# Setting up the second layer's weights beside the first layer's last feed-forward groups

## The chip, the cores and the metric

The kernel runs on one core of a Trainium2 chip. The metric is the device time of one execution in microseconds (us). Engines are called as the profile calls them: PE (TensorE; PEld is its weight load), DVE (VectorE), ACT (ScalarE), POOL (GpSimd) and SP (SyncE, which here only issues transfers).

## The reference

Two layers act on x (32 graphs of 512 nodes with 256 features, float32) with a 0/1 adjacency of 512 x 512 for each graph. Each layer adds a graph layer and a feed-forward layer, both on a layer norm of x:

```python
# layer 0
x = x + relu(mean_over_neighbours(ln(x) @ W_msg) + ln(x) @ W_upd + bias)
t = max_d(ln(x)[d] + Wt[f, d]) + bt                # "tropical" product, f = 0..1023
fused = g * bend(t) + (1 - g) * gelu(ln(x) @ Wc)   # g = sigmoid(ln(x) @ Wg), bend piecewise linear
x = x + fused @ Wd + bd
# layer 1
x = x + graph_attention(ln(x), adj)                # 4 heads of 64, softmax over neighbours
sw = softmax((ln(x) @ W_x.T + b_x) @ W_slice.T + b_slice) / temperature)   # 8 heads, 64 slices
x = x + (sw.T-weighted sums of ln(x) @ W_fx.T, mixed by a small recurrence, spread by sw) @ out_w.T
```

Before layer 1 can start, its weights are put into the form that the products want: W_fx and four other matrices are loaded by row blocks and transposed, W_x and W_slice are multiplied together, some norms are compared with limits.

## The kernel before

**Layer 0** is `layer0_sorted`. The 32 graphs form four segments of eight (segments 0 to 3). A generator `all_convs`, held in the variable `ahead`, does the graph convolution of a segment (`conv_in`, `conv_out`) and ends each segment with `put_in_order`. That function ranks all rows of the segment by how much work their tropical product needs and scatters the 32 row tiles `keep[t]` to a DRAM buffer `by_rank` in rank order, with 32 indirect DMAs on POOL's queue (L440). All these buffers come from a pool `sa`.

A second generator, `feed_forwards`, takes each sorted segment in eight groups (0 to 7). For a group, `sums` loads the rows (`xs`, L469 on SP), normalizes and transposes them, and gathers table rows on POOL (`rows`, L499) for the tropical maximum on DVE (`best`). `mixed` does the two products with Wc and Wg (clsp and gatep, L524 on PE), their ACT functions, the transposed tropical part (tz, L531) and the bends (`past` on ACT, `acc` on DVE). `down` multiplies by Wd (po, L551), adds on DVE (L553) and stores the rows to `x2s[s]` (L554 on SP). In the order of instructions, group g's `down` stands after the first step of group g+1's `mixed`, and the rest of `mixed` is interleaved with `sums` of the group after.

The two generators are interleaved by a helper, `woven(a, na, b, nb)`: it takes steps from a and b in the proportion na to nb, so the order of instructions on each engine is the order in which the generators are stepped. The stream `ahead` runs ahead by 32 steps and more; its last step, `put_in_order` of segment 3, comes while group 5 of segment 2 is begun, with eleven groups still to be finished.

**Layer 1** is `layer1_plain`, called when layer 0 is done. It opens its constants' pool `c1` and its PSUM pool `p1`, and does the setup:

- loads `wa` and, in a small pool `raw0`, the vectors a_dst and a_src (L813), which go into `wa` and a norm (`prod` on DVE, norm2p on PE, L820);
- loads some twenty small constants (L789);
- in a pool `raw`, calls `load_T` five times (L881, L882): a row block is loaded, each 128 x 128 part is transposed on PE (wfxp, inp, hop, owp, fcp: 72 in all) and copied on DVE;
- makes `wsl`, the product of W_x and W_slice (wslp, L922), compares norms, and takes the exponential of `ebsl`.

Then pools `s1` and others are opened and pairs of graphs go through attention and the slice mixer. `prepare` gathers the rows of a graph from `x2s` by their ranks (`x`, L960 on POOL), normalizes them and turns the adjacency (`ai`) into a mask; the first products of `attention` are avp (L1025).

Pools may lie on the left or the right end of the core's SBUF. A pool that is opened on memory which an earlier pool has given back waits, at its first uses, for all users of the memory given back. With `reuse_waits="tile"` a buffer waits only for those whose own bytes it takes.

Of the kernel before, what the change touches and what calls it, by code (L numbers as in the profile page):

```python
# [8 lines left out]
F32 = mybir.dt.float32  # L9
# [6 lines left out]
PSUM = bass.MemoryType.PSUM  # L16
DRAM = bass.MemoryType.DRAM

P = 128
N = 512  # L20
# [59 lines left out]
        live = [s for s in live if next(s, live) is not live]  # L80


def layer0_sorted(tc, ident, eps, x, adj, w, x2s, ranks, over):

# [3 lines left out]
    nc = tc.nc  # L90
# [22 lines left out]
    with ExitStack() as ctx:  # L113
        cst = ctx.enter_context(tc.tile_pool(name="c0", bufs=1))
# [36 lines left out]
        keys = dr.tile([FFN], F32, tag="keys", name="keys", bufs=1)  # L151
        sorted_rows = dr.tile([FFN, 4 * D + NF], F32, tag="sorted", name="sorted_rows", bufs=1)

        sa = ctx.enter_context(tc.tile_pool(name="sa", bufs=2))

        def bounds(raw):

# [411 lines left out]
        def all_convs():  # L569
            for s in range(len(x2s)):  # L570
                yield from convs(s)
                yield s

        ahead = all_convs()
        with tc.tile_pool(name="r0", bufs=1) as raw:
            bounds(raw)
            first = iter(lambda: next(ahead), 0)
            for _ in woven(first, SEG * 12, features(raw), 40):
                pass
        sb = ctx.enter_context(tc.tile_pool(name="s0", bufs=2))  # L580

        for _ in range(LEAD):
            next(ahead)
# [166 lines left out]
            feed_forward(g, xg, xnT, acc)  # L750


def layer1_plain(tc, ident, eps, x2s, ranks, adj, w, out, over):


    nc = tc.nc
# [20 lines left out]
    SMALL_S, SMALL_B = 50.0 * 50.0 / D, 20.0  # L777

    with ExitStack() as ctx:
        cst = ctx.enter_context(tc.tile_pool(name="c1", bufs=1))  # L780
        dr = ctx.enter_context(tc.tile_pool(name="d1", bufs=2, space=DRAM))
        ps = ctx.enter_context(tc.tile_pool(name="p1", bufs=4, space=PSUM))

        def ctile(name, shape):
            return cst.tile(shape, F32, tag=name, name=name)
# [4 lines left out]
            return t  # L790

        def psum(tag, name):
            return ps.tile([P, N], F32, tag=tag, name=name, bufs=4)

        ones = ctile("ones", [P, P])
        nc.gpsimd.memset(ones, 1.0)
# [6 lines left out]
        for c in range(DC):  # L803
            nc.sync.dma_start(wa[:, c, : AH * HO].rearrange("p (h e) -> p h e", h=AH),
                              w["W"][:, c * P : (c + 1) * P, :].rearrange("h p e -> p h e"))
        with tc.tile_pool(name="raw0", bufs=1) as raw:
            prod = raw.tile([P, DC, AH, HO], F32, tag="prod", name="prod")
            norm2 = raw.tile([P, DC, 2, AH], F32, tag="norm2", name="norm2")
            for i, name in enumerate(("a_dst", "a_src")):
                dst = wa[:, :, AH * (HO + i) : AH * (HO + i + 1)]  # L810
                vec = raw.tile([P, AH, HO], F32, tag=name, name=name)
                for h in range(AH):
                    nc.sync.dma_start(vec[:, h, :], w[name][h, 0, :].partition_broadcast(P))  # L813
                for c in range(DC):
                    nc.vector.tensor_mul(prod[:, c], wa[:, c, : AH * HO].rearrange("p (h e) -> p h e", h=AH), vec)
                nc.vector.tensor_reduce(dst, prod, AX.X, ALU.add)
                nc.vector.tensor_mul(norm2[:, :, i, :], dst, dst)
            pn = psum("mm", "norm2p")
            for c in range(DC):
                nc.tensor.matmul(pn[:, : 2 * AH], ones, norm2[:, c].rearrange("p i h -> p (i h)"),  # L820
                                 start=c == 0, stop=c == DC - 1)
            nc.vector.tensor_scalar(over[:, : 2 * AH], pn[:, : 2 * AH], SMALL, None, ALU.is_gt)
        edges = ctile("edges", [P, 2, B * NT])
        abias = const("abias", [P, AH * HO], w["gnn_bias"].rearrange("h e -> (h e)").partition_broadcast(P))
        gamma = const("gamma", [P, AH * HO], w["ln_gamma"].rearrange("h e -> (h e)").partition_broadcast(P))
# [41 lines left out]
        owT = ctile("owT", [P, KC, D])  # L867
        fcT = ctile("fcT", [P, KC, H])

        with tc.tile_pool(name="raw", bufs=2) as raw:  # L870

            def load_T(dst, src, name):

                R, Ccols = src.shape
                for r0 in range(0, R, P):
                    n = min(P, R - r0)
                    t = raw.tile([P, Ccols], F32, tag=f"raw{Ccols}", name=f"{name}_{r0}")
                    nc.sync.dma_start(t[:n], src[r0 : r0 + n, :])
                    for c in range(Ccols // P):
                        pt = psum("tp", f"{name}p{r0}_{c}")  # L880
                        nc.tensor.transpose(pt[:, :n], t[:n, c * P : (c + 1) * P], ident[:n, :n])  # L881
                        nc.vector.tensor_copy(dst[:, c, r0 : r0 + n], pt[:, :n])  # L882

            load_T(wfxT, w["W_fx"], "wfx")
            load_T(inT, w["hy_in_w"], "in")
            load_T(hoT, w["hy_out_w"], "ho")
            load_T(owT, w["out_w"], "ow")
            load_T(fcT, w["hy_fcD_w"], "fc")
            norm = raw.tile([P, KC], F32, tag="norm", name="norm")
            nc.sync.dma_start(norm, w["hy_norm_w"].rearrange("(c p) -> p c", p=P))  # L890
            for c in range(KC):
                nc.vector.tensor_scalar_mul(hoT[:, c, :], hoT[:, c, :], norm[:, c : c + 1])

            def twice_T(src, name):

                R, Ccols = src.shape
                t = raw.tile([P, 2, Ccols], F32, tag="twice", name=name)
                for i in range(2):
                    nc.sync.dma_start(t[:R, i, :], src)
                pt = psum("tp", f"{name}p")  # L900
                nc.tensor.transpose(pt[:, :R], t[:R].rearrange("p i c -> p (i c)"), ident[:R, :R])
                return pt


            wsT = raw.tile([P, G], F32, tag="wsT", name="wsT")
            nc.vector.tensor_copy(wsT, twice_T(w["W_slice"], "ws")[:, :G])
            wx = raw.tile([P, KC, D], F32, tag="wx", name="wx")
            nc.sync.dma_start(wx, w["W_x"].rearrange("(k p) d -> p k d", p=P))
            bx = raw.tile([P, KC], F32, tag="bx", name="bx")
            nc.sync.dma_start(bx, w["b_x"].rearrange("(k p) -> p k", p=P))  # L910
            bsl = raw.tile([1, H, G], F32, tag="bsl", name="bsl")
            bs = raw.tile([1, G], F32, tag="bs", name="bs")
            nc.sync.dma_start(bs, w["b_slice"].rearrange("(o n) -> o n", o=1))
            for c in range(DC + 1):
                M = P if c < DC else 1
                for i in range(H // KC):

                    half = slice(i * C, (i + 1) * C)
                    px = psum("mm", f"wslp{c}_{i}")
                    for k in range(KC):  # L920
                        lhs = wx[half, k, c * P : (c + 1) * P] if c < DC else bx[half, k : k + 1]
                        nc.tensor.matmul(px[:M, k * G : (k + 1) * G], lhs, wsT[half, :], start=True, stop=True)  # L922
                    px = px[:M, : KC * G].rearrange("p (k g) -> p k g", k=KC)
                    rt = rtemp[:M, i :: H // KC].unsqueeze(2).to_broadcast([M, KC, G])
                    if c < DC:
                        nc.vector.tensor_mul(wsl[:, c, i :: H // KC, :], px, rt)
                    else:
                        dst = bsl[:, i :: H // KC, :]
                        nc.vector.tensor_add(dst, px, bs.unsqueeze(1).to_broadcast([1, KC, G]))
                        nc.vector.tensor_mul(dst, dst, rt)  # L930
            wsl = wsl.rearrange("p c h g -> p c (h g)")
            nc.sync.dma_start(bsl_row.rearrange("(o n) -> o n", o=1), bsl.rearrange("p h g -> p (h g)"))
            nc.sync.dma_start(ebsl, bsl_row.partition_broadcast(P))
            pn = psum("mm", "norm2s")
            for c in range(DC):
                sq = raw.tile([P, H * G], F32, tag="wsl2", name=f"wsl2_{c}")
                nc.vector.tensor_mul(sq, wsl[:, c, :], wsl[:, c, :])
                nc.tensor.matmul(pn, ones, sq, start=c == 0, stop=c == DC - 1)
            most = raw.tile([P, 3], F32, tag="most", name="most")
            nc.vector.tensor_reduce(most[:, 0:1], pn, AX.X, ALU.max)  # L940
            nc.vector.tensor_reduce(most[:, 1:2], ebsl, AX.X, ALU.max)
            nc.vector.tensor_reduce(most[:, 2:3], ebsl, AX.X, ALU.min)
            for i, limit, op in ((0, SMALL_S, ALU.is_gt), (1, SMALL_B, ALU.is_gt), (2, -SMALL_B, ALU.is_lt)):
                nc.vector.tensor_scalar(over[:, 2 * AH + i : 2 * AH + i + 1], most[:, i : i + 1], limit, None, op)
            nc.scalar.activation(ebsl, ebsl, AF.Exp)

        sb = ctx.enter_context(tc.tile_pool(name="s1", bufs=2))

        def wide(tag, name, bufs):
            return sb.tile([P, N], F32, tag=tag, name=name, bufs=bufs)  # L950
# [939 lines left out]
def tile_kernel(ctx, tc, ins, out):  # L1890
# [21 lines left out]
    with tc.tile_pool(name="few", bufs=1) as few:  # L1912
# [1 line left out]
        NSEG = 4  # L1914
        x2s = [dram.tile([len(x2) // NSEG * N, D], F32, tag=f"x2s_{i}", name=f"x2s_{i}") for i in range(NSEG)]
        ranks = few.tile([P, len(x2) * NT], I32, tag="ranks", name="ranks")
        layer0_sorted(tc, ident, eps2, ins["x"], ins["adj"], w0, x2s, ranks, over[:, :n0])
        layer1_plain(tc, ident, eps, x2s, ranks, ins["adj"], w1, out, over[:, n0:])


        ones = few.tile([P, 1], F32, tag="ones", name="ones")
# [43 lines left out]
```

## Time and profile before

| what | us |
|---|---|
| runs: median (lowest to highest of three) | 5609.2 (5591.56 to 5611.99) |
| the profiled execution's own time | 5599.06 |
| its span | 5597.3 |
| PE busy | 4349.1 (78%) |
| DVE busy | 3780.8 (68%) |
| ACT busy | 1815.2 (32%) |
| POOL busy | 1458.0 (26%) |
| first scatter of segment 3 (L440) issued | 2224.18 |
| last scatter of segment 3 issued | 2339.75 |
| stores of segment 2, groups 4 to 7 (L554) | 2238.14, 2300.17, 2359.76, 2429.50 |
| last store of layer 0 | 2859.41 |
| first avp of layer 1 | 2958.85 |

The mean granted PE clock is 0.86 of full speed. Times of instructions are from the start of the span of one profiled execution; busy time is the sum over the instructions of an engine, so the busy shares are averages over parts of the kernel that have different limits. "Idle before" an instruction is put down to the semaphore event that came last.

### The profile page before, as it was taken

The page shows a single profiled execution, that of the slowest core. Times are in us where ns is not written, and L with a number is a line of the kernel's source. Part 1 is how long each engine was busy: PE and PEld are TensorE (multiplying, and loading weights), DVE is VectorE, ACT ScalarE, POOL GpSimd, SP SyncE. Part 2 cuts the span into 40 slices and gives each one's busy share as a digit, 9 for nine tenths or more (in the row PEclk, how much of TensorE's full clock was granted, in tenths as well). Part 3 has the DMA queues.
Part 4 walks back from the last instruction along what each step waited for, and adds up shares of the span by engine and source line. Part 5 has one row for each costly group of instructions (what it writes and reads, how often), then busy time and mean ns, then how long its engine had stood idle before and what let it go on. Part 6 is the DMA issues. An engine that isn't in the chain of part 4 may idle for free.

```text
span 5597.3 us, 59701 instructions
## 1 busy us (share of the span) xinstructions
PE 4349.1 (78%) x20723; PEld 3036.2 (54%) x20723; DVE 3780.8 (68%) x8934; ACT 1815.2 (32%) x3827; POOL 1458.0 (26%) x1658
## 2 busy tenths in 40 slices
PE   5565887867877778879968778788777878877787
PEld 3442554544554555445546666566566656656664
DVE  7667776878868777687856565665665566565553
ACT  1102332423333333434524233333333333333332
POOL 2244334333344333443311111111111111111110
PEclk8787988989998899989976888889888888888888
DMA  3325333344334333454422110111111011111100
GB/s 106 113 79 199 110 125 115 126 150 136 121 114 150 131 106 99 142 193 133 132 88 67 33 38 29 42 46 46 44 33 38 31 38 46 46 44 33 35 20 13
DMA packets 235116, 474.32 MB, mean 85 GB/s; under 512 B 38299, under 2 KB 114075, under 8 KB 234804
## 3 DMA queue, kind: packets, MB, share of 16 engines
q0 software_dynamic: 80256, 282.38, 15.4%
q1 hardware_dynamic: 154548, 188.02, 10.9%
q8 instruction: 166, 2.72, 0.2%
q14 instruction: 146, 1.20, 0.1%
HBM read 413.16 MB, written 57.16 MB: 84 GB/s over the span
## 4 chain that ended last, share of the span: by engine, by line
PE 31%; DVE 10%; ACT 6%; DMA 4%; issue 4%; POOL 3%; SPq 0%; DVEq 0%; POOLq 0%; ACTq 0%
PE avp L1025 9%; PE lgp L1071 3%; PE outp L1296 3%; PE yTp L1083 2%; PE oTp L1276 2%; PE zp L1128 2%; POOL sw L1073 1%; PE xp L1135 1%; DMA rows<-table,xs 1%; DVE att L1019 1%; PE vp L1287 1%; ACT swT L1090 1%; PE yp L1245 1%; PE po L551 1%; PE hp L990 1%
## 5 line engine op out<-in xcount | busy, mean ns | idle before, releaser
L1019 DVE SCALAR_TENSOR_TENSOR att<-own,other,mask 128x512 f32<-128x512 f32 x512 | 404.2, 803 | 346.0 <-PE avp L1025 336.8
L524 PE MATMUL clsp<-xnT,wc 128*128 128x512 f32 x1024 | 540.8, 646 | 107.1 <-ACT gate L526 72.5
L1025 PEld LDWEIGHTS avp<-hv,att 128*128 128x128 f32 x4096 | 522.1, 208 | 25.8 <-issue 14.4
L551 PE MATMUL po<-wd,acc 128*128 128x256 f32 x2048 | 484.2, 394 | 61.3 <-DVE acc L542 23.6
L1025 PE MATMUL avp<-hv,att 128*128 128x65 f32 x4096 | 525.5, 291 | 6.0 <-DVE att L1019 5.9
L499 POOL DMA_INDIRECT rows<-table,xs x332 | 409.7, 1234 | 426.3 <-DVE best L503 165.4
L524 PE MATMUL gatep<-xnT,wg 128*128 128x512 f32 x1024 | 496.0, 603 | 0.1
L551 PEld LDWEIGHTS po<-wd,acc 128*128 128x128 f32 x2048 | 398.6, 198 | 142.6 <-DVE xs L553 30.6
L538 DVE SCALAR_TENSOR_TENSOR acc<-past,fld,acc 128x512 f32<-128x512 f32 x448 | 353.0, 791 | 43.2 <-ACT past L537 34.2
L960 POOL DMA_INDIRECT x<-x2s,ranks x128 | 134.3, 1049 | 915.2 <-DVE rs L1030 632.3
L533 ACT ACTIVATE acc<-tz,fld 128x512 f32<-128x512 f32 x256 | 198.9, 777 | 482.8 <-PE tz L531 419.9
L531 PE MATMUL tz<-ident,best 128*128 128x128 f32 x1024 | 179.9, 291 | 202.4 <-DVE best L505 164.4
L505 DVE SCALAR_TENSOR_TENSOR best<-rows,xs,best 128x1024 f32<-128x1024 f32 x212 | 273.5, 1290 | 88.1 <-DMA rows<-table,xs 86.9
L524 PEld LDWEIGHTS clsp<-xnT,wc 128*128 128x128 f32 x1024 | 189.9, 204 | 263.6 <-issue 121.2
L524 PEld LDWEIGHTS gatep<-xnT,wg 128*128 128x128 f32 x1024 | 198.3, 197 | 230.8 <-issue 203.6
L526 ACT ACTIVATE gate<-gatep,fld 128x512 f32<-128x512 f32 x256 | 175.9, 687 | 431.7 <-DVE acc L541 238.2
L381 PE MATMUL pm<-h,adj 128*128 128x257 f32 x1024 | 279.6, 415 | 39.8 <-DVE u L387 26.0
L531 PEld LDWEIGHTS tz<-ident,best 128*128 128x128 f32 x1024 | 130.2, 147 | 326.0 <-DVE best L505 150.8
L537 ACT ACTIVATE past<-tz,fld 128x512 f32<-128x512 f32 x448 | 289.5, 692 | 28.6 <-DVE acc L538 27.6
L526 ACT ACTIVATE cls<-clsp,fld 128x512 f32<-128x512 f32 x256 | 176.2, 688 | 353.8 <-DVE acc L542 171.0
L1071 PE MATMUL lgp<-wsl,x4T 128*128 128x512 f32 x512 | 263.1, 649 | 35.7 <-ACT x4T L57 21.6
L381 PEld LDWEIGHTS pm<-h,adj 128*128 128x128 f32 x1024 | 206.7, 208 | 104.7 <-issue 32.8
(381 smaller groups left out, 8676.2 us busy)
## 6 DMA issues: line engine op xcount, KB each, us to landing
adji<-in_adj SPq DMA_DIRECT2D x128, 256.0 KB, 2.9
ai<-in_adj SPq DMA_DIRECT2D x128, 256.0 KB, 2.7
own<-ownd SPq DMA_DIRECT2D x128, 256.0 KB, 3.7
xs<-by_rank SPq DMA_DIRECT2D x32, 550.0 KB, 3.9
x<-in_x SPq DMA_DIRECT2D x32, 512.0 KB, 4.9
x2s<-xs SPq DMA_DIRECT2D x32, 512.0 KB, 2.9
out<-x SPq DMA_DIRECT2D x32, 512.0 KB, 2.9
rows<-table,xs POOLq DMA_INDIRECT x332, 5.5
```

The costliest lines, as they stand in the source:

```text
L381: nc.tensor.matmul(pm[:, : D + 1], a[:, i, t * P : (t + 1) * P], h[:, i, :], start=i == 0, stop=i == NT - 1)
L499: nc.gpsimd.indirect_dma_start(out=row, out_offset=None, in_=table, in_offset=bass.IndirectOffsetOnAxis(ap=idxs[:, k : k + 1].bitcast(U32) ...
L505: nc.vector.scalar_tensor_tensor(m, row, vals[:, k : k + 1], m, ALU.add, ALU.max)
L524: nc.tensor.matmul(pf, wf[:, c, f * P : (f + 1) * P], xnT[:, c, :], start=c == 0, stop=c == DC - 1)
L526: nc.scalar.activation(o, pf, fn, bias=fld[:, f, bf : bf + 1], scale=1.0 if fn == AF.Gelu else 0.5)
L531: nc.tensor.transpose(pt[:, t, :], best[t][:, f * P : (f + 1) * P], ident)
L537: nc.scalar.activation(r, z, AF.Relu, bias=fld[:, f, AT + b : AT + b + 1])
L538: nc.vector.scalar_tensor_tensor(y, r, fld[:, f, CH + b : CH + b + 1], y, ALU.mult, ALU.add)
L551: nc.tensor.matmul(po[:, :D], acc[f][:, t * P : (t + 1) * P], wd[:, f, :], start=f == 0, stop=f == FC - 1)
L1019: nc.vector.scalar_tensor_tensor(e, own[h], other[:, j, h : h + 1], mask[:, j, :], ALU.max, ALU.mult)
L1025: nc.tensor.matmul(pv[:, t * HE : (t + 1) * HE], att[j][:, t * P : (t + 1) * P], hv[:, j, h, :], start=j == 0, stop=j == NT - 1)
L1071: nc.tensor.matmul(pf, xnT[:, c, t * P : (t + 1) * P], wsl[:, c, :], start=c == 0, stop=c == DC - 1)
```

## The change

The pool `sa` goes to the right end of SBUF and is closed when the stream of convolutions ends. The stream then goes on with the setup of layer 1, so that the setup's instructions are interleaved with the feed-forward groups that remain. For that, `layer1_plain` becomes a generator: it yields after the a_dst/a_src part, after each row block of `load_T` and each part of `wsl`, and yields True when the setup is done; its remainder is run after `layer0_sorted`. Its setup takes PSUM buffers from layer 0's pool (`ps`, two buffers for each tag). Its pools `c1`, `raw0` and `raw` lie at the right end, in the memory that `sa` gave back. `c1`, `s0`, `s1` and `p1` get `reuse_waits="tile"`; `raw0` and `raw` keep the default waits. `load_T` puts up to four transposes into one PSUM buffer and copies them with one ACT instruction.

```diff
-        sa = ctx.enter_context(tc.tile_pool(name="sa", bufs=2))
+        aside = ctx.enter_context(ExitStack())
+        sa = aside.enter_context(tc.tile_pool(name="sa", bufs=2, side="right"))
...
             for s in range(len(x2s)):
                 yield from convs(s)
                 yield s
+            aside.close()
+            yield from following(ps)
...
-        sb = ctx.enter_context(tc.tile_pool(name="s0", bufs=2))
+        sb = ctx.enter_context(tc.tile_pool(name="s0", bufs=2, reuse_waits="tile"))
...
-def layer1_plain(tc, ident, eps, x2s, ranks, adj, w, out, over):
+def layer1_plain(tc, ident, eps, x2s, ranks, adj, w, out, over, ps):
...
-        cst = ctx.enter_context(tc.tile_pool(name="c1", bufs=1))
+        cst = ctx.enter_context(tc.tile_pool(name="c1", bufs=1, side="right", reuse_waits="tile"))
-        ps = ctx.enter_context(tc.tile_pool(name="p1", bufs=4, space=PSUM))
...
-            return ps.tile([P, N], F32, tag=tag, name=name, bufs=4)
+            return ps.tile([P, N], F32, tag=tag, name=name)
...
-        with tc.tile_pool(name="raw0", bufs=1) as raw:
+        with tc.tile_pool(name="raw0", bufs=1, side="right") as raw:
...
             nc.vector.tensor_scalar(over[:, : 2 * AH], pn[:, : 2 * AH], SMALL, None, ALU.is_gt)
+        yield
...
-        with tc.tile_pool(name="raw", bufs=2) as raw:
+        with tc.tile_pool(name="raw", bufs=2, side="right") as raw:
...
-                    for c in range(Ccols // P):
-                        pt = psum("tp", f"{name}p{r0}_{c}")
-                        nc.tensor.transpose(pt[:, :n], t[:n, c * P : (c + 1) * P], ident[:n, :n])
-                        nc.vector.tensor_copy(dst[:, c, r0 : r0 + n], pt[:, :n])
+                    pt = psum("tp", f"{name}p{r0}").rearrange("p (c r) -> p c r", r=P)
+                    cs = Ccols // P
+                    for c in range(cs):
+                        nc.tensor.transpose(pt[:, c, :n], t[:n, c * P : (c + 1) * P], ident[:n, :n])
+                    nc.scalar.copy(dst[:, :, r0 : r0 + n], pt[:, :cs, :n])
+                    yield
...
                         nc.vector.tensor_mul(dst, dst, rt)
+                yield
...
-        sb = ctx.enter_context(tc.tile_pool(name="s1", bufs=2))
+        yield True
+        ps = ctx.enter_context(tc.tile_pool(name="p1", bufs=4, space=PSUM, reuse_waits="tile"))
+        sb = ctx.enter_context(tc.tile_pool(name="s1", bufs=2, reuse_waits="tile"))
...
-        layer0_sorted(tc, ident, eps2, ins["x"], ins["adj"], w0, x2s, ranks, over[:, :n0])
-        layer1_plain(tc, ident, eps, x2s, ranks, ins["adj"], w1, out, over[:, n0:])
+        rest = []
+
+        def following(ps):
+            rest.append(layer1_plain(tc, ident, eps, x2s, ranks, ins["adj"], w1, out, over[:, n0:], ps))
+            return iter(lambda: next(rest[0]), True)
+
+        layer0_sorted(tc, ident, eps2, ins["x"], ins["adj"], w0, x2s, ranks, over[:, :n0], following)
+        for _ in rest[0]:
+            pass
```

More of the change, by code (lines that the diff above doesn't have):

```diff
@@ L80, in braid, with layer0_sorted @@
         live = [s for s in live if next(s, live) is not live]
-def layer0_sorted(tc, ident, eps, x, adj, w, x2s, ranks, over):
+def layer0_sorted(tc, ident, eps, x, adj, w, x2s, ranks, over, following):
     nc = tc.nc
@@ L878, in load_T @@
                     nc.sync.dma_start(t[:n], src[r0 : r0 + n, :])
-                    for c in range(Ccols // P):
-                        pt = psum("tp", f"{name}p{r0}_{c}")
-                        nc.tensor.transpose(pt[:, :n], t[:n, c * P : (c + 1) * P], ident[:n, :n])
-                        nc.vector.tensor_copy(dst[:, c, r0 : r0 + n], pt[:, :n])
[L884 to L888, printed above, removed]
+                    pt = psum("tp", f"{name}p{r0}").rearrange("p (c r) -> p c r", r=P)
[4 more added lines that the diff above has]
+                    yield
+            yield from load_T(wfxT, w["W_fx"], "wfx")
+            yield from load_T(inT, w["hy_in_w"], "in")
+            yield from load_T(hoT, w["hy_out_w"], "ho")
+            yield from load_T(owT, w["out_w"], "ow")
+            yield from load_T(fcT, w["hy_fcD_w"], "fc")
             norm = raw.tile([P, KC], F32, tag="norm", name="norm")
```

## The prediction

> **What bounds the kernel now.** I read the windows around the place where layer 1 begins, then the chain of waits, then the queues of GpSimd (POOL) and SyncE (SP) where the setup is to go. First the windows (us, busy time of PE, PEld, DVE, ACT, POOL with counts, PEclk, DMA share, GB/s):
>
> ```profile
> 2238.00:2300.00 62.00, 47.84 (x163) 28.91 (x162) 40.87 (x59) 21.36 (x34) 34.63 (x32) 0.89 0.46 148
> 2810.00:2862.00 52.00, 48.01 (x177) 30.25 (x175) 30.98 (x50) 22.59 (x36) 2.04 (x10) 1.00 0.08 26
> 2862.00:2890.00 28.00, 9.21 (x36) 6.55 (x36) 10.84 (x44) 1.49 (x2) 0.00 (x0) 0.53 0.49 127
> 2890.00:2920.00 30.00, 20.25 (x97) 14.31 (x97) 15.27 (x60) 0.00 (x0) 0.00 (x0) 0.50 0.26 77
> ```
>
> The last feed-forward groups keep PE 92% busy at full clock; the next 58 us have PE busy for 29.5, at half clock. That is layer 1's setup. The chain of waits names its limit:
>
> ```profile
> 2862.01 5.39 DMA beta<-in_L_gnn_ln_beta
> 2870.77 4.80 DMA wfx<-in_L_ffn_W_fx
> 2880.47 2.84 DMA in<-in_L_ffn_hy_in_w
> 2883.45 1.10 PE inp L881 x4
> 2910.97 5.66 PE wslp L922 x43
> 2924.67 0.96 POOL x L960
> 2958.85 6.29 PE avp L1025 x32
> ```
>
> Weights arrive in 2.6 to 2.8 us, two row blocks in flight, and 1.1 us of transposes lies between. The setup runs from 2858.9 to 2924.0, **65 us**, and another 34.9 pass until the first attention product (avp).
>
> Where the setup is to go, POOL does the scatters of the last sort:
>
> ```profile
> 2224.18 1.02 POOL L440 DMA_INDIRECT by_rank<-keep,ranks  x1 [14.68 <-DVE ranks L438]
> 2227.07 1.01 POOL L440 DMA_INDIRECT by_rank<-keep,ranks  x1 [1.86 <-DMA by_rank<-keep,ranks]
> 2229.97 0.97 POOL L440 DMA_INDIRECT by_rank<-keep,ranks  x1 [1.90 <-DMA by_rank<-keep,ranks]
> 2232.75 0.97 POOL L440 DMA_INDIRECT by_rank<-keep,ranks  x1 [1.81 <-DMA by_rank<-keep,ranks]
> ```
>
> Each scatter waits until the one before has landed. And SP, around that time:
>
> ```profile
> 2238.14 0.36 SPq L554 DMA_DIRECT2D x2s<-xs  x1
> 2241.39 0.36 SPq L469 DMA_DIRECT2D xs<-by_rank  x1
> 2342.80 1.30 SPq L813 DMA_DIRECT2D a_dst<-in_L_gnn_a_dst  x3
> ```
>
> The a_dst load of layer 1 already leaves in mid-layer 0, and only when the 32nd scatter (issued at 2339.75) has landed: its pool raw0 lies where the conv's buffers lay. It hurts nobody, as SP has no urgent work behind it.
>
> [...]
>
> **The change part by part.**
>
> *1. The setup leaves the boundary.* Minus 65. The layer-1 prologue follows the last store directly. Its 34.9 us contain 16 gathers of x (L960) at 1.25 us, from 2924.7 to 2938.1 and landing some 3 us later, which POOL could issue only after the setup (it waited 63.4 us for "over"). In the changed program they stand after the last row gathers of the feed-forward, on a POOL that is busy for 2 of 52 us; so they are done by its end, and what held ACT's third layer norm to 2942.2 is gone. The adjacency loads (2.7 to 5.4 us each, two in flight) then set the pace: about 28 us. Minus 6 or 7. Together **−71**; bounds −64 (prologue no quicker) and −80 (14 of the 34.9 go).
>
> *2. The setup beside groups 5 to 7 of segment 2 (both counted from 0).* The conv stream ends with the 32 scatters; at its next step the pool is closed and raw0 opened on it. raw0 kept its default waits, so its a_dst loads wait for all users of the given-back bytes: the last scatters. New is what is queued behind. In the changed program:
> - POOL has all 32 scatters back to back, ahead of the memset of "ones" and of group 6's row gathers. 2224.2 + 31 × 2.88 (the spacing above) = 2313.5, landed 2.7 later: **2316**. From 2.78 apiece: 2313; at segment 0's 3.34 ((426.54 − 323.09)/31, conv work between them): 2330.
> - SP has behind a_dst: a_src, some twenty small constants, the first row blocks of weights, group 4's store (L554) and group 6's load (L469).
> - PE has norm2p (L820), which needs ones, a_dst and a_src, ahead of po of group 4 (L551) and all later work; DVE has prod (L815) ahead of group 4's adds and group 5's acc; ACT waits for the temperature load ahead of group 5's "past".
>
> PE's work before norm2p (clsp and gatep of 5_0 to 5_2) ends near 2231. So **all four engines stand from 2231 to 2316 and beyond**. Then: eight a_dst/a_src loads (3.5 us to issue, 2.9 to land) 2322.6; prod, sums, norm2p, 2324.6; small loads on SP (10 us of issue in the old setup) until 2330, first wfx block landed (4.8 to 5.2) 2335.5, for which PE stops in mid-po; the remaining 20 po matmuls at 0.44 us, 2345; group 4's store 2346 instead of 2238.1: +108.
>
> After that some comes back. From 2238 to 2430 PE was busy 155 of 192 us (62, 60 and 70 us of windows: 47.8, 51.8, 55.5), so 37 were free; the setup's PE work, 29.5 at half clock, takes 15 to 20. A stretch bound by PE alone would regain 17 to 22; DVE (64 of 70 us busy in group 7), the weight loads in pairs of 4 us and head-of-line transposes leave about half: −8. **Shift of the feed-forward's end: +100**, bounds +85 (all regained, short scatters) and +125 (3.34 per scatter, nothing regained).
>
> *3. load_T with one copy on ACT for up to four transposes.* 72 DVE copies of 0.29 us (21 us of DVE) become 20 ACT copies. ACT is 36 to 43% busy there: nothing. ACT loads two tables more and Gelu's again, 1.28 each: hidden by the same slack[...].
>
> *4. Tile waits of s0, c1, s1, p1.* The first xs load at 429.2 follows the last scatter of segment 0 (426.54 plus landing) in both: nothing at the start. s1 and p1 are in part 1. No other order changes in the steady layers. From 2960 to 3040 the clock is 0.50 with PE 79% busy; I expect that to stay[...].
>
> **Sum**: 100 − 71 = **+29** on the profiled execution's own 5599.06: 5628. That one lies 10 below the median of 5609.2 (runs 5591.6 to 5612.0), from which it would be 5638. Between them, **5633**. About 0.5% (28 us) is what a measurement of this kernel can tell from no change.
>
> **Rivals.**
> - *The wait is short, and the kernel faster* (the other side). If scatters without row gathers among them went faster, the stall would shrink: the gain of 71 pays for a shift of 71, reached when the spacing is (2316 − 29 − 2.7 − 2224.2)/31 = 1.94 us or less. For: POOL is busy 1.0 us per scatter, and the row gathers follow one another at 1.25. At 1.27, 32 of them land by 2266, and the net is −21 (5588 by the median). If the wait were met in time altogether, the setup would hide in PE's 37 free us and leave −71 + 15 = −56 (5553). Against: four consecutive spacings of 2.8 to 2.9 with the releaser "DMA by_rank", and 95 waits on it in the whole trace. 0.14 for both.
> - *The stall spreads.* Nothing comes back, the weight loads come serially after the stall, and group 6, whose gathers also stand behind the scatters, ends up with +125 to +130: net +55 to +60, 5664 to 5669. For: SP issues in order, and group 6's load waits for group 4's store. Against: PE's free share later. 0.22.
> - *The setup doesn't move.* If the waits put the setup's bulk after the last group anyway, only the stall or only a few us remain: within ±15 of 5609. Against: the stream's steps are drawn by the weave, eight groups before the end. 0.06.
> - The forecast itself, +10 to +45: 0.58.
>
> **How the numbers follow.** The forecast's own range is 5615 to 5655; with the spread of the two bases and the spread rival it goes to 5672; downwards to 5588, the short-wait case. Slower by over 0.5% (above 5637): somewhat over half of the forecast's case (0.34 of 0.58) and the spread rival (0.22), 0.56. Within: the rest of the forecast and the unmoved setup, 0.30. Faster: the short wait, 0.14.
>
> **What would show it.** Right: PE, DVE and ACT idle from about 2231 to 2320, put down to a_dst, a_src or by_rank; 32 scatters at 2.9 us without a gather between them; group 4's store near 2346; gathers of x before the last po; first avp some 28 us after the last x2s store, without wfxp, inp and wslp between. Wrong: scatters closer than 2 us; group 4's store before 2270; the last store less than 75 us later than 2859.4; or a prologue that is as long as before.

## The result, and the profile after

The changed kernel takes 5635.8 us (median of four runs, 5634.9 to 5642.0) against 5606.3 of the kernel before measured beside it (four runs, 5591.6 to 5612.0): a ratio of **1.0059, 95% interval 1.0038 to 1.0080**. The forecast was 5633. The profiled execution has a span of 5640.2 us against 5597.3, and the difference of 42.9 us can be read in three parts (from here on, "the first avp" is the very first of these products on PE, at 2955.15 in the kernel before; the 2958.85 of the table ahead of the prediction is a later one):

| stretch | before | after | difference |
|---|---|---|---|
| start to the last store of layer 0 | 2859.4 | 2960.9 | +101.5 |
| last store to the first avp | 95.7 | 27.0 | −68.7 |
| first avp to the end | 2642.2 | 2652.3 | +10.1 |

The first row is the stall. These are windows of the changed kernel (us, busy time of PE, PEld, DVE, ACT, POOL with counts, PEclk, DMA share, GB/s):

```profile
2222.00:2228.00 6.00, 5.91 (x15) 2.35 (x13) 0.00 (x0) 2.66 (x3) 2.25 (x3) 1.00 0.13 48
2228.00:2323.00 95.00, 0.00 (x0) 0.00 (x0) 3.18 (x8) 0.00 (x0) 30.87 (x40) 0.51 0.15 51
2323.00:2343.00 20.00, 18.32 (x74) 15.34 (x74) 4.43 (x13) 4.71 (x10) 0.00 (x0) 0.84 0.37 90
2343.00:2396.00 53.00, 47.90 (x191) 30.41 (x192) 39.78 (x59) 27.22 (x45) 19.42 (x15) 0.94 0.55 172
```

For 95 us PE and ACT do nothing at all and DVE works for 3 us, while POOL is busy for a third of the time. POOL's timeline (start, duration, idle time before and its releaser) says with what:

```profile
2222.02 1.02 POOL L441 DMA_INDIRECT by_rank<-keep,ranks  x1 [14.87 <-DVE identb L803]
2224.81 0.99 POOL L441 DMA_INDIRECT by_rank<-keep,ranks  x1 [1.77 <-DMA by_rank<-keep,ranks]
...
2312.29 0.97 POOL L441 DMA_INDIRECT by_rank<-keep,ranks  x1 [2.26 <-DMA by_rank<-keep,ranks]
2313.26 0.22 POOL L799 MEMSET ones<- 128x128 f32 x1
```

Thirty-two scatters without a row gather among them, 90.3 us from the first to the last: 2.91 us each, of which 1.0 is busy. Only then do SP's loads leave, and PE's next matmul (norm2p) runs at 2323.3. SP:

```profile
2315.01 1.76 SPq L816 DMA_DIRECT2D a_dst<-in_L_gnn_a_dst  x4
...
2343.15 0.37 SPq L555 DMA_DIRECT2D x2s<-xs  x1
2346.09 0.36 SPq L470 DMA_DIRECT2D xs<-by_rank  x1
```

The store at 2343.15 is that of group 4 (2238.14 before), and the load at 2346.09 that of group 6 (2241.39 before). The waits between 2228 and 2345 (total, times, longest) put a name on each engine:

```profile
ACT nega L844 <- DMA nega<-in_L_ffn_hy_A_log: 105.6, 1, 105.6
DVE prod L818 <- DMA a_src<-in_L_gnn_a_src: 97.7, 1, 97.7
...
PE norm2p L823 <- DMA beta<-in_L_gnn_ln_beta: 95.3, 1, 95.3
POOL by_rank L441 <- DMA by_rank<-keep,ranks: 58.4, 30, 2.7
```

ACT, DVE and PE have a single wait of some 100 us each; the longest single wait of the kernel before in this stretch is 30.1 (ACT). PE's is put down to beta, which is merely the load that landed last before norm2p; the chain behind it is scatters, a_dst, a_src, prod, norm2p.

The second row is the gain. The chain of waits at the boundary has no setup in it:

```profile
2949.70 10.64 PE po L552 x48
...
2961.29 4.98 DMA ai<-in_adj
...
2982.70 0.72 ACT a L981 x2
...
2984.73 6.04 DMA ai<-in_adj
...
2991.97 6.83 PE avp L1034 x32
```

The adjacency load follows the last store at once. The gathers of x no longer appear, because all 16 ran before it, four near 2910 and twelve from 2946:

```profile
2946.22 0.94 POOL L969 DMA_INDIRECT x<-x2s,ranks  x1 [31.09 <-PE gatep L525]
...
2960.05 0.95 POOL L969 DMA_INDIRECT x<-x2s,ranks  x1 [0.30 <-issue]
```

### The profile page after: what moved, and what is told of

Same layout as the page of the kernel before. It is cut to its first block, busy times and chain, and to the rows that moved or that the text cites. A ratio compares the mean times of both kernels' runs of the same rounds, so it can differ in the third digit from the quotient of the medians.

```text
span 5640.2 us, 59620 instructions
## 1 busy us (share of the span) xinstructions
PE 4351.9 (77%) x20723; PEld 3038.5 (54%) x20723; DVE 3762.2 (67%) x8858; ACT 1828.3 (32%) x3851; POOL 1465.4 (26%) x1658
## 4 chain that ended last, share of the span: by engine, by line
PE 38%; DVE 20%; DMA 15%; issue 11%; POOL 9%; ACT 7%; SPq 0%; POOLq 0%; DVEq 0%; ACTq 0%
PE avp L1034 9%; DMA rows<-table,xs 6%; DMA by_rank<-keep,ranks 4%; PE lgp L1080 3%; PE po L552 3%; POOL rows L500 3%; PE outp L1305 3%; PE yTp L1092 2%; DMA rows<-table,tops 2%; DVE acc L539 2%; PE pm L382 2%; PE zp L1137 2%; PE oTp L1285 2%; POOL xs L481 1%; POOL sw L1082 1%
## 5 line engine op out<-in xcount | busy, mean ns | idle before, releaser
L382 PEld LDWEIGHTS pm<-h,adj 128*128 128x128 f32 x1024 | 208.8, 211 | 102.8 <-issue 32.2
```

Source lines behind the costliest of these rows:

```text
L382: nc.tensor.matmul(pm[:, : D + 1], a[:, i, t * P : (t + 1) * P], h[:, i, :], start=i == 0, stop=i == NT - 1)
```

## The experiments

The first scatter of segment 3 starts anywhere from 2207 to 2224 us in these traces; in the two of the kernel before alone it starts at 2224.2 and 2209.7. So places are compared from that scatter on; all numbers are from the profiled executions, the time and ratio from all runs (one run for e1 and e8).

| kernel | first scatter to last store | last store to first avp | first avp to end | time | ratio to before (95%) |
|---|---|---|---|---|---|
| before | 635.2 | 95.7 | 2642.2 | 5606.3 | |
| e8, before again | 637.0 | 96.4 | 2653.5 | 5598.4 | |
| changed | 738.9 | 27.0 | 2652.3 | 5635.8 | 1.0059 (1.0038 to 1.0080) |
| e1 | 739.0 | 26.1 | 2652.0 | 5631.4 | |
| e2 | 706.1 | 26.7 | 2653.0 | 5599.2 | 0.9987 (0.9974 to 1.0000) |
| e3 | 709.5 | 26.5 | 2653.9 | 5599.3 | 0.9987 (0.9979 to 0.9996) |
| e4 | 681.6 | 27.0 | 2650.9 | 5576.5 | 0.9943 (0.9925 to 0.9962) |
| e5 | 668.7 | 27.5 | 2649.7 | 5560.7 | 0.9915 (0.9896 to 0.9933) |
| e6 | 673.5 | 26.8 | 2655.7 | 5571.2 | 0.9941 (0.9919 to 0.9963) |
| e7 | 643.9 | 77.4 | 2645.3 | 5592.5 | 0.9976 (0.9968 to 0.9984) |
| e9 | 664.3 | 26.6 | 2649.7 | 5555.8 | 0.9922 (0.9902 to 0.9941) |
| e10 | 665.5 | 27.2 | 2659.4 | 5561.7 | 0.9932 (0.9913 to 0.9950) |

The theory: engines stand because the setup's first buffer takes bytes that the last scatter still reads, and, beside that, because ones is set on POOL behind the scatters. The rivals: the shift is the setup's own work beside busy groups; or it is the default waits as such (for all users of the memory given back, whichever bytes are taken).

**e1, tile waits for raw0 and raw.**

```diff
-        with tc.tile_pool(name="raw0", bufs=1, side="right") as raw:
+        with tc.tile_pool(name="raw0", bufs=1, side="right", reuse_waits="tile") as raw:
...
-        with tc.tile_pool(name="raw", bufs=2, side="right") as raw:
+        with tc.tile_pool(name="raw", bufs=2, side="right", reuse_waits="tile") as raw:
```

> The changed kernel with tile waits for raw0 and raw too. Theory (the stall is the wait of raw0's bytes for the last scatters, and of the memset of ones behind them on POOL): raw0 happens to lie on the bytes of keep[31], the last to be scattered, so even its own bytes' users hold the a_dst load until about 2315; PE stands from 2228 to about 2323, group 4's store stays near 2343, the last store near 2961, time 5636 (5625 to 5645). Rival (the stall is due to the default waits for all users of the given-back memory, as the change's name suggests): a_dst leaves near 2225, group 4's store comes near 2245, and the time falls by 80 or more, to about 5555.

Nothing moved: 739.0 us to the last store, as in the changed kernel. SP's timeline of e1:

```profile
2305.85 1.95 SPq L816 DMA_DIRECT2D a_dst<-in_L_gnn_a_dst  x4
...
2334.38 0.37 SPq L555 DMA_DIRECT2D x2s<-xs  x1
```

a_dst leaves 93.4 us after the first scatter (2212.48), against 93.0 in the changed kernel. A wait for one's own bytes is no shorter where those bytes are the ones that come free last. The kind of wait is out as the cause in this layout; default waits with the other layout of e2 were not tried.

**e2, other bytes, and ones on DVE.** The keep buffers in reverse order, so that raw0 lies on the one that is scattered first.

On top of e1's edit:

```diff
-            keep = [sa.tile([P, RW], F32, tag=f"keep{t}", name=f"keep{s}_{t}", bufs=1) for t in range(ST)]
+            keep = [sa.tile([P, RW], F32, tag=f"keep{t}", name=f"keep{s}_{t}", bufs=1) for t in reversed(range(ST))][::-1]
...
-        nc.gpsimd.memset(ones, 1.0)
+        nc.vector.memset(ones, 1.0)
```

> As e1, with the keep buffers laid out in reverse, so that raw0 lies on keep[0], the first to be scattered, and raw on keep[14] to keep[21]; and with the memset of ones on DVE instead of POOL. Theory: a_dst leaves near 2228 and norm2p runs near 2235; the next wait is the first wfx block's, for the scatter of keep[21] (issued 2222 + 21 x 2.88 = 2282, landed 2285); PE stands in po of group 4 from about 2240 to 2290 instead of 2228 to 2323; group 4's store near 2305 instead of 2343; last store near 2922; time about 5598 (5585 to 5612). Rival (the shift of 101 us is the setup's own work and the loads beside the groups): last store stays near 2961, time 5636.

SP's and PE's timelines of e2:

```profile
2215.31 1.95 SPq L816 DMA_DIRECT2D a_dst<-in_L_gnn_a_dst  x4
...
2281.05 0.80 SPq L882 DMA_DIRECT2D wfx<-in_L_ffn_W_fx  x2
...
2296.03 0.37 SPq L555 DMA_DIRECT2D x2s<-xs  x1
```

```profile
2227.52 0.99 PE L823 MATMUL norm2p<-norm,ones 128*128 128x8 f32 x4 [8.88 <-DVE norm L820]
...
2283.00 0.69 PE L886 MATMUL wfxp<-ident,wfx 128*128 128x128 f32 x2 [46.46 <-DMA wfx<-in_L_ffn_W_fx]
```

a_dst left at once, and the stall became two: 8.9 us at norm2p and 46.5 at the first transpose of W_fx, which stands in the midst of group 4's po. The wfx load was issued at 2281, when the scatter of keep[21] had landed, as foreseen. With the same work in the same place PE's two waits are 40 us shorter than the one before, and 33 us of the shift are gone (739 to 706): the wait is shown as a cause of at least that much, and own work as the whole cause is out. Reversal and ones were not tried apart.

**e3, twelve empty steps.**

```diff
+            for _ in range(12):
+                yield
             aside.close()
             yield from following(ps)
```

> The changed kernel with twelve empty steps before the conv pool is closed: the setup begins one group later, beside group 6 of segment 2, while the scatters, with row gathers among them, end near 2340. Theory: PE stands from about 2298 to 2350, 50 us instead of 95; shift of the last store about 50 to 60 instead of 101 (near 2915); time 5635.8 - 45 = about 5590 (5578 to 5605). Rival (own work): the same shift of 101, time 5636.

The longest waits of PE and DVE in e3, from 2270 to 2345:

```profile
PE norm2p L825 <- DMA beta<-in_L_gnn_ln_beta: 40.4, 1, 40.4
DVE prod L820 <- DMA a_dst<-in_L_gnn_a_dst: 37.2, 1, 37.2
```

The stall shrank from 95 to 40 us. But the shift shrank only to 73 (709.5 against 636, the mean of before's two traces) where 50 to 60 were expected: some 30 us of it are something else.

**e4, twenty-four empty steps** (the edit as in e3, with 24).

> The same with twenty-four empty steps: the setup begins beside group 7, near 2360, after the last scatter has landed at 2343. Theory: no engine stands for the scatters; the setup's PE work of 15 to 20 us and some head-of-line waits shift the last store by 5 to 25 (2865 to 2885); the gain of 72 at the boundary stays; time about 5549 (5535 to 5570), a ratio of 0.990 to before. Rival (own work): last store near 2961, time 5636.

Only 5.4 us of stall are left at norm2p and the kernel is faster than before, but 45 us are left of the shift where 5 to 25 were expected, and the time is above the expected 5570. I took 20 of them for a rest of the same wait, since PE stood from 2333 to 2352 and a_dst left at 2342. e6 says otherwise.

**e5, forty empty steps** (with 40).

> The changed kernel with forty empty steps before the conv pool is closed. In e4 (24 steps) DVE still stood at prod from about 2333 and PE behind it until 2364, because the a_dst load left at 2342; the last store was 41 us late. Theory: with the setup's first part behind group 7, after 2400, nothing stands for the scatters any more, and only the setup's own work is left: last store 15 to 25 us later than before's 2859.4 (2875 to 2885), first avp 27 us after it, time 2880 + 27 + 2652 (first avp to the end, as in the five changed kernels so far) + 2 = 5561 (5550 to 5572). Rival (the 41 us of e4 are the setup's own work beside busy groups): last store near 2900, time 5580 or more, as segment 3's groups leave PE less room.

Time as expected; the last store 33 us late instead of 15 to 25.

**e6, e2's layout with twenty-four steps.**

> e2's layout (keep in reverse, tile waits for raw0 and raw, ones on DVE) with e4's twenty-four empty steps. Theory: every byte that the setup takes is free when it asks, a_dst leaves near 2300, DVE and PE don't stand near 2333 to 2364, and the shift falls from e4's 41 us to 15 to 25: last store 2875 to 2885, time 5561 (5550 to 5572). Rival (own work): last store stays near 2900, time 5577.

It came only to 673.5, 8 us below e4 and 37 above the kernel before, where 15 to 25 were expected. The first line is e6's SP, the second e6's DVE, the third e4's DVE:

```profile
2289.38 2.06 SPq L818 DMA_DIRECT2D a_dst<-in_L_gnn_a_dst  x4
```

```profile
2340.36 0.80 DVE L504 TENSOR_SCALAR best<-rows,xs 128x1024 f32<-128x1024 f32 x1 [18.88 <-DMA rows<-table,xs]
```

```profile
2350.11 0.75 DVE L504 TENSOR_SCALAR best<-rows,xs 128x1024 f32<-128x1024 f32 x1 [18.56 <-DMA rows<-table,xs]
```

Counted from the first scatter the a_dst load of e6 left 42 us earlier than e4's, and DVE stands as long at the same place, with PE behind it: for a row gather of group 7, which stands behind the last scatters in POOL's queue. My reading of e4 was wrong. The kernel before has the same gathers in the same queue, and its DVE stands there too, but only 5.7 and 12.4 us in its two traces.

**e7, the setup not moved** (300 empty steps, so that it comes after the last group; the tile waits, sides and load_T stay).

> The changed kernel with so many empty steps that the setup comes after the last feed-forward group, as before; the tile waits, the side of the pools and load_T's ACT copies stay. It tells what the move alone brings. Theory: no shift of the last store (2855 to 2865); of the 72 us gained at the boundary only what the x gathers and load_T give is left, 5 to 12 us: first avp 88 to 95 us after the last store instead of 99.4; time about 5603 (5590 to 5615). Rival (the gain comes from the waits by bytes, not from the move): first avp within 60 us of the last store, time near 5570.

The boundary took 77.4 us, less than the 88 to 95 expected (84 to 91 when counted to the very first avp). Its chain:

```profile
2859.38 0.34 SPq L884
...
2860.25 3.79 DMA wfx<-in_L_ffn_W_fx
...
2869.73 2.66 DMA in<-in_L_ffn_hy_in_w
2872.52 1.10 PE inp L888 x4
2873.64 2.77 DMA in<-in_L_ffn_hy_in_w
```

A row block still takes 3.9 us, 2.7 of load and 1.1 of transposes, so load_T's new form brings nothing to speak of. The first wfx leaves at the last store and not 11 us after it as before: with tile waits the small constants had been loaded from 2343 on, in SP's free time. The setup ends 54.8 us after the last store (64.5 before), the gathers of x are done by then, and the first adjacency load leaves 4.8 us ahead of that end. From that load to the first avp it is 27.4 us (31.1 before, where it leaves at the setup's end). So of the 69 us gained at the boundary, some 18 come without the move of PE's work and 50 come with it. That the 18 are due to the waits by bytes is argued; no run takes these away alone.

The last store is 8 us late here too. But e7 is not free of the setup in mid-layer 0: a part of it runs there all the same. On DVE:

```profile
2354.29 0.42 DVE L820 TENSOR_TENSOR prod<-wa,a_dst 128x256 f32<-128x256 f32 x1
...
2360.18 0.17 DVE L849 TENSOR_SCALAR rtemp<-rtemp 128x8 f32<-128x8 f32 x1 [3.45 <-DMA rtemp<-in_L_ffn_temperature]
```

In the kernel before, prod runs at 2861.19. From 24 empty steps on it runs 132 to 139 us after the first scatter, in e7 as in e5 or e9: so the steps do not move this first part on DVE, nor its loads on SP (a_dst leaves 123.6 us after the first scatter in e4 and e5, 123.4 in e7, 117.6 in e9), and the order on these two is not that of the generators alone. POOL, too, does the memset of ones and eight small mask operations (2.4 us) after the last scatter, ahead of the row gathers. The 8 us arise there, at group 6, where PE stands 18.1 us behind the row gather of group 7; in the two traces of the kernel before it stands 5.6 and 12.4. How much of that is the setup's first part, and how much chance, stays open.

**e8, the kernel before once more.**

> The kernel before, for a second trace of layer 1. In the first trace five of the fifteen pair periods were 160.6 us and the others 163.6 to 165; in the changed kernel's only one is below 163.7, which is 14 us from the first avp to the end (2638 against 2652). Theory (the phase of the clock at the last head's avp in a pair is chance, not the change): this trace has periods of both lengths, or mostly the long one, and first avp to the end is between 2638 and 2654, most likely near 2646. Rival (the change makes layer 1 slower, by the places of its buffers): again 2638 or less.

2653.5 us from first avp to end, within what chance was to give. (The expectation's 2638 to 2654 were counted from the avp at 2958.85; from the first they are 2642 to 2658.) So nothing says that layer 1 of the changed kernel is slower: 2645 to 2659 in the ten traces with the changed layer 1, 2642 and 2653 in the two without.

**e9, sixty-four empty steps; e10, e2's layout with forty.**

> Sixty-four empty steps: the setup beside groups 1 to 5 of segment 3, where before's PE is 81 to 98% busy and its DVE 74 to 83%. From the first scatter to the last store the kernel before took 635.2 and 637.0 us in its two traces, e7 (setup not moved) 643.9, e5 (40 steps) 668.7. Theory (what is left of the shift in e5 is the setup's own work on PE and DVE, 22 us, and 8 to 11 us that e7 shows too without the move): the own work stays, as PE has no more room there; 664 to 672 us from first scatter to last store, time near 5560 (5550 to 5572). Rival (e5's 22 us are waits of its place, behind group 7, and not work): 645 to 652, time near 5542.

> e5's forty steps with e2's layout (keep in reverse, tile waits for raw0 and raw, ones on DVE). Theory: by then the scatters have landed, so whose bytes raw0 takes is of no effect; first scatter to last store 664 to 671, time within 6 us of e5's 5560.7. Rival (the byte waits still cost where the setup starts late): 660 or less, time 5552 or less.

e9 has 664.3 and e10 665.5, both where the theory put them. A setup whose PE work comes two groups later costs no less than one behind group 7: of the 28 to 33 us left in e5, e9 and e10, e7 shows 8, and 20 to 25 us remain for the rest of the setup. In e9 this rest lies wholly behind group 7 of segment 2, so it can be read without a subtraction of e7. From that group's store to the last store, in the kernel before and in e9:

```profile
2429.50:2859.41 429.91, 384.93 (x1319) 223.74 (x1319) 332.81 (x492) 199.72 (x315) 145.25 (x118) 0.96 0.39 126
2421.42:2873.29 451.87, 402.43 (x1452) 237.46 (x1452) 340.43 (x514) 212.49 (x338) 161.78 (x131) 0.96 0.42 136
```

The columns are those of the windows further up. The stretch is 22 us longer, and PE is busy 17.5 us longer: **some 22 us are the setup's own work**, most of it PE's, the rest idle time of PE. With a setup that starts late enough, whose bytes raw0 takes has no effect that shows. e9 and e5 beat both kernels, by 0.8% against before.

## Why the prediction was right

The sum was right, 5633 against 5635.8, and nearly every term. That the two lie within 3 us of each other is partly luck: the runs of the kernel before alone spread over 20 us, and the two main terms as the traces have them, +102.8 and −68.7, would make +34 rather than +29. Term by term:

- *The scatters.* 2.88 us each predicted, 2.91 measured; the last issued 89.3 us after the first predicted, 90.3 measured. The rival's 1.94 or less was far off, since each waits for the landing of the one before (58.4 us in 30 waits).
- *What stands behind.* a_dst 2316 predicted, 2315.0; norm2p 2324.6, 2323.3; group 4's store +108, +105.0, or +107.2 counted from the first scatter. The default waits, which the step named as the reason, decide nothing in this layout: e1 shows that the bytes' own users hold the load just as long. The step said rightly that the last scatters are what is waited for. In its details, ACT stood for the load of A_log (nega) and not for the temperature's, and PE did not stop in mid-po for the first wfx block: its wait there was 0.4 us.
- *What comes back.* −8 predicted, about −4 measured (107.2 at group 4's store, 102.8 at the last store). "A stretch bound by PE alone would regain 17 to 22" left the setup's PE work at 15 to 20 us; e9 shows 17.5 of PE and some 22 in all.
- *The boundary.* −71 predicted, −68.7 measured. The setup's 65 went; the prologue gave 4 (31.1 to 27.0) instead of 6 to 7; the adjacency loads are what its chain waits for, as the step said. The absolute 34.9 and 28 were counted to the chain's avp line at 2958.85, which is not the first avp; in that count it is 31.1 after. The step read the 16 gathers of x as ending at 2938.1, where the chain leaves POOL; at 1.25 us each they went on to 2944.6. No term rests on that.
- *load_T and the ACT tables.* Nothing predicted; for load_T e7's row blocks agree (the parts are 76 transposes and 21 copies, not 72 and 20). From the first scatter to the last store ACT loads its tables four times, 1.28 us each, and not once before; what that costs was not measured apart, and in e9 it is inside the 22 us.
- *Tile waits.* What the step missed is that the small constants are loaded early: some 10 us of the 65 need no move of PE's work. In the sum it makes no difference, as all of the 65 went.
- *Layer 1.* Nothing predicted. The 10 us in the profiled pair are within what two traces of the kernel before differ by, as e8 shows; the medians differ by 29.5, and the sum was +29.

Of the rivals, "the stall spreads" would have put the last store at +125 to +130; it stood at +101.5.

## What to carry to other kernels

Work moved ahead into a gap takes its queue places along: here norm2p held PE for 95.3 us, with group 4's po behind it, and group 4's store came 105 us later. Before moving it, ask what its first instruction on every engine waits for, and what stands behind that instruction. A buffer that waits only for its own bytes' users is free no sooner if those are the last to finish (e1's a_dst left 93.4 us after the first scatter, against 93.0); choose the bytes, or start the work some steps later, which here turned +0.6% into −0.8%. And price the moved work at what it takes from the engines where it goes: here some 22 of the 50 us that the move brings.

## What the runs showed of the hardware

A pair of graphs in layer 1 takes mostly 160.6 or 163.8 us from its first store to that of the next pair, and the two traces of the kernel before differ in their mix: of the first fourteen of these periods four are 160.6 to 160.7 in one, and three are 160.6 to 160.9 in the other (e8). Two pairs of the kernel before, the same 32 matmuls of a pair's last head:

```profile
3269.55 3.77 PE L1025 MATMUL avp<-hv,att 128*128 128x65 f32 x32
...
3429.84 6.61 PE L1025 MATMUL avp<-hv,att 128*128 128x65 f32 x32
```

They run once at full and once, for the most part, at half clock (granted 1.00 and 0.54), and DVE waited 2.6 us for the first and 5.4 us for the second; the pair that follows the first store (3169.47) takes 160.6 us and the next 163.6. In the traces of the kernel before and of the changed one the granted clock is 1.00 or 0.50, and in each the 233 intervals from one change to the next are whole multiples of 3.413 us (in the kernel before 10.24, 10.24, 23.89, 3.41, 20.48 ...). What sets the place of these changes, and so the clock that a group of matmuls meets, was not shown. The long period was 163.84 us three times in the changed kernel, which is 48 times 3.413; from these two numbers I estimate that it would tend to repeat, as each such pair meets the changes at the place where the one before met them, but no run tests it. And PE's idle time, as the profile counts it, does not by itself tell where the clock is low: in the 3 us before the second group of matmuls (3426.80 to 3429.80) PE counts as busy throughout, at clock 1.00, and from 3430.35 to 3436.50, with PE as busy, it is 0.50.
